# A four-layer graph network on one core: larger first loads on two queues, masks transposed by TensorE, and transfer issues costed anew in the kernel's own schedule

## Chip, cores, metric

One core of one Trainium2 chip. The metric is the device time of one launch in microseconds; lower is better. Each number quoted for a kernel is the median of its runs. The granted TensorE clock is given with each profiled run; all runs of this study were in the fast state (none of them over 1.5% above its kernel's fastest).

## The reference, cut to what matters

32 batches of x (512 nodes, 256 channels, fp32) go through four layers. They share one 512 x 512 adjacency (1 edge in 16, int32). Each layer's result is added to its input and normalised.

```python
def reference(x, adj, ...):
    x = _layernorm(x + _L0_gnn_ref(x, adj, w_qkv, ...))   # 8-head attention, layernorm, FFN, layernorm
    x = _layernorm(x + _L1_gnn_ref(x, W, a, adj))         # 1-head graph attention
    x = _layernorm(x + _L2_gnn_ref(x, adj, W1, W2, W3))   # product attention: (x W1)(x W2)^T
    x = _layernorm(x + _L3_gnn_ref(x, adj, W, a))         # 4-head graph attention, elu
    return x                                              # each attention masked by adj > 0
```

## The kernel before

The kernel does not write its instructions in source order. Every operation is first recorded with a *modelled* cost for each engine that could do it. Then a greedy list scheduler simulates the core and emits the operations in the order in which it placed them. Five batches are open at once. A modelled cost is never executed; it only decides the order of the instructions in each engine's queue, and (where two engines could do an operation) which does it.

```python
AGE = 30.0
LAT = {"PE": 0.3, "DVE": 0.15, "ACT": 0.2, "POOL": 0.25, "SP": 4.0}   # us until a result is usable
# ... (in Plan.run)
            tmin = min(c[0] for c in cands)                  # earliest possible start
            s, o, e = min((c for c in cands if c[0] <= tmin + 0.05),
                          key=lambda c: (not c[1].frees, c[1].graph * AGE - c[1].rank))
            # ...
            if emit:
                o.fn(e)                                      # the instruction is emitted here
            # ...
            for n in o.succ:
                n.ready = max(n.ready, f + LAT[e])
```

The evacuation of a PSUM bank (the copy of PE's result, `ps`, to a tile that other operations read; DVE or ACT may do it) and the layernorm, whose scales come from a chain of four small instructions on POOL (GpSimd):

```python
    def evac(ps, dst, part, out, src=lambda b: b.t, n=512):          # L339 is the copy on ACT
        op({"DVE": cdve(n), "ACT": cact(n)}, lambda e: copy(e, out(dst), src(ps)),
           r=[ps], w=[dst[part]])
    # ... layernorm
            op({"POOL": 1.6}, scales, r=[mv], w=[mv])                # L426 to L429
            # ...
                op({"DVE": 0.325, "ACT": cact(C, 2)}, norm, r=[y[s], mv], w=[dst[s]])   # L438 on ACT
```

Layers 1 and 3 spread their node scores over all partitions by way of DRAM: four stores of rows, then one or two broadcast loads. DVE needs those loads before it can build the matrices that layer 3's products use. Afterwards the products are transposed back:

```python
        def put(e):
            for i in range(4):                               # four DMAs
                nc.sync.dma_start(rd..., rt.t[32 * i:32 * i + n1, :32])
        op({"SP": 0.4}, put, r=[rt], w=[rd])
        for s in range(len(R)):
            op({"SP": 0.2}, lambda e, s=s: nc.sync.dma_start(
                T2(R[s])[:, :hs, :], rd.t[2 * s:2 * s + hs].partition_broadcast(P)), r=[rd], w=[R[s]])
    # ... layer3, after the products (L764 and L770) have been evacuated into sT and oT
        op({"PE": 4 * TR}, back_s, r=[sT], w=[ps_r])         # L785: the sums, transposed back
        # ...
            op({"PE": 4 * TR}, back, r=[oT], w=[ps_t], pre=[t])      # L801: the values
```

The loads at the start, all from SP. The adjacency comes twice: once in 16 block-permuted DMAs for the transposed mask, once in natural rows:

```python
        def block(e, b=b, xZ=xZ):                            # x of one batch, 8 DMAs
            for i in range(4):
                for k in range(KC):
                    nc.sync.dma_start(T2(xZ)[32 * i:32 * i + 32, k, :]..., v[i, :, k])
        op({"SP": 0.8}, block, w=[xZ])
    # ... mask_cols, twice: 8 DMAs of 64 KB, convert on ACT, transpose and compare on DVE
            op({"SP": 0.8}, fn, w=[z])
    # ... mask_rows, per 128 rows
            op({"SP": 0.1}, load(lambda z=z: T2(z)[:, 0, :].bitcast(I32), adj[c * P:(c + 1) * P, :]), w=[z])
            op({"ACT": cact(512) + 0.1}, ... activation(T2(f)[:, 0, :], ..., AF.Copy, accum_out=...), ...)
```

## Time and profile before

| | before |
|---|---|
| median (range), 3 runs | 3114.74 us (3114.32 to 3115.23) |
| profiled span, granted clock | 3116.0 us, 0.983 |
| PE busy | 2967.7 us (95%) |
| start of layer 3's back transposes, first batch | 258.77 us |
| the same, from batch to batch: first six | 97.67, 96.28, 97.28, 97.52, 98.77, 94.8 us |
| the same, settled | 92.4 to 93.0 us; 95.65 and 93.88 once each |

The last rows come from the order of time on PE: I take the start of L785 in each of the 32 batches and subtract. The prediction below shows the page, the table of stretches and the first 60 us.

### The profile page before, as it was taken

To read this page: it belongs to the slowest core of one execution; us is meant where nothing else is said; L and a number is where in the kernel's file an instruction comes from. 1 tells how busy PE (TensorE), PEld (TensorE's weight loads), DVE (VectorE), ACT (ScalarE), POOL (GpSimd) and SP (SyncE) were. 2 spreads that over 40 slices of the span, in tenths; PEclk is the share of its full clock that TensorE was granted. 3 is DMA by queue.
4 is the path that set the end of the run, shared out by engine and by line. 5 is a ranking of instruction groups with operands and counts; after the bars stand their busy time and mean duration, and the time that the engine had idled before them with its cause. 6 is when DMAs were issued, how large, how long until landed. Compare 5 with 4: busy or idle time off the path is not lost. (4 is left out here: it accounts for less than half of the span.)

```text
span 3116.0 us, 49565 instructions
## 1 busy us (share of the span) xinstructions
PE 2967.7 (95%) x17882; PEld 1633.4 (52%) x17882; DVE 2641.2 (85%) x5283; ACT 1693.9 (54%) x3473; POOL 957.2 (31%) x1809
## 2 busy tenths in 40 slices
PE   6899999999999999999999999999999999999885
PEld 2355545555555555455555555555555555555553
DVE  5988888788998888898888998888898888899853
ACT  3555555655555555555555555655555655556342
POOL 0223232232332333333333233333233333233311
PEclk8899999999999999999999999999999999999997
DMA  7001101101011111101101101101101101100000
GB/s 142 12 20 26 38 24 32 38 21 38 25 31 38 29 31 38 31 25 38 38 21 38 38 18 38 38 21 38 38 18 38 38 21 38 38 21 28 31 25 29
DMA packets 205244, 103.76 MB, mean 33 GB/s; under 512 B 154432, under 2 KB 191808, under 8 KB 204992
## 3 DMA queue, kind: packets, MB, share of 16 engines
q1 hardware_dynamic: 204992, 100.52, 12.5%
q8 instruction: 143, 2.34, 0.3%
q14 instruction: 109, 0.89, 0.1%
HBM read 83.36 MB, written 17.12 MB: 32 GB/s over the span
## 5 line engine op out<-in xcount | busy, mean ns | idle before, releaser
L438 ACT ACTIVATE b<-b,t 128x256 f32<-128x256 f32 x768 | 434.2, 600 | 523.4 <-POOL t L429 507.4
L339 ACT ACTIVATE b<-ps 128x512 f32<-128x512 f32 x772 | 430.7, 601 | 361.6 <-PE ps L367 144.1
L485 DVE TENSOR_TENSOR b<-b,maskT 128x1024 f32<-128x1024 f32 x512 | 596.5, 1212 | 16.0 <-ACT b L479 16.0
L479 ACT ACTIVATE b<-ps 128x512 f32<-128x512 f32 x1024 | 527.2, 607 | 128.1 <-PE ps L474 128.1
L426 POOL TENSOR_SCALAR t<-t 128x2 f32<-128x2 f32 x384 | 166.3, 433 | 972.5 <-DVE t L421 873.1
L756 DVE SCALAR_TENSOR_TENSOR b<-b,s,maskT 128x512 f32<-128x512 f32 x512 | 359.1, 741 | 10.7 <-DMA b<-r 10.6
L427 POOL TENSOR_TENSOR t<-t,mhalf 128x2 f32<-128x2 f32 x384 | 339.0, 883 | 32.0
L474 PE MATMUL ps<-b,b 32*128 32x512 f32 x2048 | 301.8, 640 | 21.0 <-ACT b L339 21.0
L497 DVE TENSOR_TENSOR b<-b,b 128x1024 f32<-128x1024 f32 x256 | 297.5, 1210 | 0.0
L419 DVE BATCH_NORM_STATS2 t<-b 128x6 f32<-128x256 f32 x768 | 283.5, 411 | 6.7
L764 PE MATMUL ps<-b,b 128*64 128x512 f32 x1024 | 241.6, 609 | 20.3 <-DVE b L756 20.3
L379 PE MATMUL ps<-b,wqkv_sb 128*128 128x512 f32 x512 | 250.3, 614 | 9.8 <-DMA wqkv_sb<-in_L_gnn_w_qkv_dram 9.8
L407 POOL TENSOR_TENSOR acc<-acc,s 128x32 f32<-128x32 f32 (+2 forms) x96 | 48.2, 502 | 688.2 <-DVE s L524 423.3
L729 PE MATMUL ps<-b,b 128*128 128x257 f32 x1024 | 233.0, 384 | 20.1 <-ACT b L339 20.0
L466 PE MATMUL ps<-b,b 128*32 128x512 f32 x2048 | 247.4, 601 | 0.0
L702 PE MATMUL ps<-b,b 128*128 128x512 f32 x512 | 240.6, 592 | 0.0
L396 PE MATMUL ps<-w_sb,b 128*128 128x256 f32 x1024 | 238.8, 386 | 0.0
L669 PE MATMUL ps<-b,b 128*128 128x257 f32 x1024 | 229.7, 380 | 4.4 <-DVE b L660 4.4
L379 PE MATMUL ps<-b,w_sb 128*128 128x512 f32 x512 | 230.5, 602 | 0.0
L729 PEld LDWEIGHTS ps<-b,b 128*128 128x128 f32 x1024 | 192.3, 190 | 54.4 <-ACT b L339 27.0
L710 DVE CUSTOM_DVE_ANT_0 b<-ps,b 128x512 f32<-128x512 f32 x128 | 87.3, 682 | 149.7 <-ACT b L706 149.7
L669 PEld LDWEIGHTS ps<-b,b 128*128 128x128 f32 x1024 | 193.2, 189 | 38.5 <-issue 5.3
(124 smaller groups left out, 4174.9 us busy)
## 6 DMA issues: line engine op xcount, KB each, us to landing
b<-r SPq DMA_DIRECT2D x64, 512.0 KB
b<-in_x_dram SPq DMA_DIRECT2D x256, 64.0 KB
b<-in_x_dram SPq DMA_DIRECT2D x32, 512.0 KB
out_dram<-b SPq DMA_DIRECT2D x64, 256.0 KB
b<-r SPq DMA_DIRECT2D x32, 256.0 KB
r<-s SPq DMA_DIRECT2D x128, 0.5 KB
r<-s SPq DMA_DIRECT2D x128, 2.0 KB
b<-in_adj_dram SPq DMA_DIRECT2D x16, 64.0 KB
```

What stands on the lines that cost most here:

```text
L339: nc.scalar.activation(dst, src, AF.Copy)
L379: nc.tensor.matmul(ps.t, w.t[:, i, col + k * P:col + (k + 1) * P], T2(xT)[:, i, :], start=(i == 0), stop=(i == KC - 1))
L419: nc.vector.bn_stats(st.t[:, 6 * j:6 * j + 6], T4(y)[:, 2 * s + j, :])
L427: nc.gpsimd.tensor_tensor(mv.t[:, 6:8], mv.t[:, 4:6], mhalf[:, :2], ALU.pow)
L438: nc.scalar.activation(o, i, AF.Identity, bias=b, scale=sc)
L474: nc.tensor.matmul(s[h].t, T2(kT)[r:r + D0, g, c * P:(c + 1) * P], T2(qT)[r:r + D0, g, :], start=True, stop=True)
L479: op({"ACT": cact(512)}, lambda e, c=c, j=j, i=i, s=s, p=p: nc.scalar.activation(T2(p[j][c])[:, i, :], s[2 * j + i].t, AF.Exp, scale=SC0), ...
L485: nc.vector.tensor_tensor(t, t, maskT[c].t.unsqueeze(1).to_broadcast([P, 2, N]), ALU.mult)
L497: op(TT, lambda e, a=p[j][c - 1], b=p[j][c]: nc.vector.tensor_tensor(T2(a), T2(a), T2(b), ALU.add), r=[p[j][c - 1], p[j][c]], w=[p[j][c - 1]])
L669: nc.tensor.matmul(ps.t[:, :C + 1], T2(p[m // 2])[:, m % 2, c * P:(c + 1) * P], hv.t[:, m * (C + 1):(m + 1) * (C + 1)], start=(m == 0), st ...
L729: nc.tensor.matmul(ps_o.t[:, :C + 1], T2(pT)[:, j, m * P:(m + 1) * P], vv()[:, m, :], start=(m == 0), stop=(m == NC - 1))
L756: nc.vector.scalar_tensor_tensor(T2(b)[:, h % 2, :], T2(R[h // 2])[:, h % 2, :], part(1)[:, 0, m, h:h + 1], maskT[m].t, ALU.max, ALU.mult),
```

## The change

Its intent: get the first projection and the masks going sooner with fewer, larger DMAs issued from SP and ACT; load the adjacency once, in natural rows, and have TensorE transpose it; and cost every transfer issue in the schedule at 0.53 us, where the old numbers meant 0.1 (row stores, x) to 0.4. Cut to its core:

```diff
+    DMA = 0.53
 ...
-        op({"SP": 0.4}, put, r=[rt], w=[rd])                  # four row stores, layers 1 and 3
+        op({"SP": 4 * DMA}, put, r=[rt], w=[rd])
 ...
-            op({"SP": 0.2}, lambda e, s=s: nc.sync.dma_start( # row loads
+            op({"SP": DMA}, lambda e, s=s: nc.sync.dma_start(
 ... xs, out, and every constant's load: SP 0.1 / 0.2 / 0.4 -> DMA or n * DMA
-                (nc.sync).dma_start(dst(), src)
+                (nc.scalar if e == "ACT" else nc.sync).dma_start(dst(), src)
 ...
-    def mask_cols(): ...        # 16 block DMAs, 2 DVE transposes, 4 compares
-    def mask_rows(): ...        # 4 row DMAs on SP
+    def masks():
+        for c in range(NC):
+            op({"ACT": DMA}, load(..., adj[c * P:(c + 1) * P, :]), w=[z])
+            op({"ACT": cact(512) + 0.1}, ... parts4(edges(c)), swap(...), AF.Copy, accum_out=...)
+        for m in range(NC):
+            op({"PE": 4 * TR}, tr, r=f, w=[ps])               # 4 transposes of 128x128
+            evac(ps, maskT[m], None, lambda b: b.t)
 ...
-            op({"SP": 0.3}, load(lambda: wqkv_sb.t, rows(w_qkv)), w=[wqkv_sb])
+            op({"ACT": DMA}, load(lambda: wqkv_sb.t, rows(w_qkv)), w=[wqkv_sb])
 ...
             for i in range(4):
-                for k in range(KC):
-                    nc.sync.dma_start(T2(xZ)[32 * i:32 * i + 32, k, :]..., v[i, :, k])
-        op({"SP": 0.8}, block, w=[xZ])
+                nc.sync.dma_start(T2(xZ)[32 * i:32 * i + 32]..., v[i])
+        op({"SP": 4 * DMA}, block, w=[xZ])
```

So the change has two halves: the transfers (what is loaded, by whom, in how many pieces, and the masks) and the model (the numbers in the braces).

More of the change, by code (lines that the diff above doesn't have):

```diff
@@ L505, in layer0 @@
             if g == 0:
-                op({"SP": 0.1}, lambda e: nc.sync.dma_start(
+                op({"SP": DMA}, lambda e: nc.sync.dma_start(
                     T4(xs), x[b].rearrange("(c p) d -> p c d", p=P)), r=[oT[0]], w=[xs])
@@ L823, in fn @@
             with nc.allow_non_contiguous_dma(reason="constants, once"):
-                nc.sync.dma_start(dst(), src)
+                (nc.scalar if e == "ACT" else nc.sync).dma_start(dst(), src)
         return fn
@@ L831, in cols @@
         return a.rearrange("(k p) -> p k", p=P)
-    def mask_cols():
-        for k in range(0, NC, 2):
-            z, f = Buf("B"), Buf("B")
-            def fn(e, k=k, z=z):
-                v = adj.rearrange("(j b) (i k a) -> i b k j a", b=32, k=NC, i=4)
-                for i in range(4):
-                    for q in range(2):
-                        nc.sync.dma_start(
-                            T2(z)[32 * i:32 * i + 32, q, :].bitcast(I32).rearrange(
-                                "p (j a) -> p j a", a=32), v[i, :, k + q])
-            op({"SP": 0.8}, fn, w=[z])
-            op({"ACT": cact(1024)}, lambda e, z=z, f=f: nc.scalar.activation(
-                f.t[:, :2 * N], z.t[:, :2 * N].bitcast(I32), AF.Copy), r=[z], w=[f])
-            z2 = Buf("B")
-            op({"DVE": cdve(1024)}, lambda e, z2=z2, f=f: nc.vector.transpose(
-                z2.t[:, :2 * N], f.t[:, :2 * N]), r=[f], w=[z2])
-            for q in range(2):
-                op({"DVE": 0.35}, lambda e, q=q, k=k, z2=z2: nc.vector.tensor_scalar(
-                    maskT[k + q].t, T2(z2)[:, q, :], 1.0, None, ALU.is_equal), r=[z2], w=[maskT[k + q]])
@@ L855, in mask_rows, with edges, tr @@
-    def mask_rows():
-        cnt = Buf("T")
+    def masks():
+        cnt, f = Buf("T"), [Buf("B"), Buf("B")]
+        def edges(c):
+            return T2(f[c // 2])[:, c % 2, :]
         for c in range(NC):
-            z, f = Buf("B"), Buf("B")
-            op({"SP": 0.1}, load(lambda z=z: T2(z)[:, 0, :].bitcast(I32), adj[c * P:(c + 1) * P, :]),
+            z = Buf("B")
+            op({"ACT": DMA}, load(lambda z=z: T2(z)[:, 0, :].bitcast(I32), adj[c * P:(c + 1) * P, :]),
                w=[z])
-            op({"ACT": cact(512) + 0.1}, lambda e, c=c, z=z, f=f: nc.scalar.activation(
-                T2(f)[:, 0, :], T2(z)[:, 0, :].bitcast(I32), AF.Copy,
-                accum_out=cnt.t[:, c:c + 1]), r=[z], w=[f, cnt])
-            op({"DVE": 0.35}, lambda e, c=c, f=f: nc.vector.tensor_scalar(
-                maskN.t[:, c, :], T2(f)[:, 0, :], 0.0, -BIG, ALU.is_le, ALU.mult),
-                r=[f], w=[maskN])
-            op({"DVE": 0.7}, lambda e, c=c, f=f: nc.vector.tensor_tensor_reduce(
-                T2(f)[:, 1, :], T2(f)[:, 0, :], T2(f)[:, 0, :], 1.0, 0.0, ALU.mult, ALU.add,
-                cnt.t[:, NC + c:NC + c + 1]), r=[f], w=[f, cnt])
+            op({"ACT": cact(512) + 0.1}, lambda e, c=c, z=z: nc.scalar.activation(
+                parts4(edges(c)), swap(T2(z)[:, 0, :].bitcast(I32)), AF.Copy,
+                accum_out=cnt.t[:, c:c + 1]), r=[z], w=[f[c // 2][c % 2], cnt[c]])
+        for m in range(NC):
+            ps = Buf("PS")
+            def tr(e, m=m, ps=ps):
+                for c in range(NC):
+                    nc.tensor.transpose(ps.t[:, c * P:(c + 1) * P],
+                                        edges(c)[:, m * P:(m + 1) * P], ident)
+            op({"PE": 4 * TR}, tr, r=f, w=[ps])
+            evac(ps, maskT[m], None, lambda b: b.t)
+        scr = Buf("B")
+        for c in range(NC):
+            op({"DVE": 0.6}, lambda e, c=c: nc.vector.tensor_scalar(
+                swap(maskN.t[:, c, :]), parts4(edges(c)), 0.0, -BIG, ALU.is_le, ALU.mult),
+                r=[f[c // 2][c % 2]], w=[maskN])
+            op({"DVE": 0.62}, lambda e, c=c: nc.vector.tensor_tensor_reduce(
+                T2(scr)[:, 0, :], edges(c), edges(c), 1.0, 0.0, ALU.mult, ALU.add,
+                cnt.t[:, NC + c:NC + c + 1]), r=[f[c // 2][c % 2]], w=[scr, cnt[NC + c]])
@@ L884, in ffn_weights @@
         for dst, src in ((w1_sb, w1), (w2_sb, w2)):
-            op({"SP": 0.1}, load(lambda d=dst: d.t, rows(src)), w=[dst])
+            op({"SP": DMA}, load(lambda d=dst: d.t, rows(src)), w=[dst])
         for dst, src in ((b1_sb, b1), (g1c, ln1_g), (be1c, ln1_b)):
-            op({"SP": 0.1}, load(lambda d=dst: d.t, cols(src)), w=[dst])
+            op({"SP": DMA}, load(lambda d=dst: d.t, cols(src)), w=[dst])
         for dst, src in ((g1_sb, ln1_g), (g2_sb, ln2_g), (be2_sb, ln2_b)):
-            op({"SP": 0.1}, load(lambda d=dst: d.t, src.partition_broadcast(P)), w=[dst])
+            op({"SP": DMA}, load(lambda d=dst: d.t, src.partition_broadcast(P)), w=[dst])
         for dst, src in ((be1r, ln1_b), (b2r, b2)):
-            op({"SP": 0.1}, load(lambda d=dst: d.t[:, :C], src.partition_broadcast(P)), w=[dst])
+            op({"SP": DMA}, load(lambda d=dst: d.t[:, :C], src.partition_broadcast(P)), w=[dst])
         ps = Buf("PS")
@@ L922, in put @@
                     nc.sync.dma_start(c1p.t[i:i + 1, k, :], bf(i)[0:1, :])
-            op({"SP": 0.2}, put, r=[parts[i]], w=[c1p])
+            op({"SP": 2 * DMA}, put, r=[parts[i]], w=[c1p])
     def score_weights(w, src, a, heads):
@@ L931, in score_weights @@
         for j in range(4):
-            op({"SP": 0.4}, load(lambda j=j: w.t[32 * j:32 * j + 32, :, :C],
+            op({"SP": DMA}, load(lambda j=j: w.t[32 * j:32 * j + 32, :, :C],
                                  src.rearrange("(q a) d -> a q d", a=32)), w=[w])
-        op({"SP": 0.4}, load(lambda: wr.t[:, :KC * C].rearrange("p (k d) -> p k d", k=KC), rows(src)),
+        op({"SP": DMA}, load(lambda: wr.t[:, :KC * C].rearrange("p (k d) -> p k d", k=KC), rows(src)),
            w=[wr])
-        op({"SP": 0.4}, load(lambda: a_sb.t[:, :n], a.partition_broadcast(P)), w=[a_sb])
+        op({"SP": DMA}, load(lambda: a_sb.t[:, :n], a.partition_broadcast(P)), w=[a_sb])
         def fn(e):
@@ L951, in put @@
                                   sc.t[:, :KC * e3].rearrange("p (k e) -> p k e", k=KC))
-        op({"SP": 0.4}, put, r=[sc], w=[dr])
+        op({"SP": DMA}, put, r=[sc], w=[dr])
         def get(e):
@@ L958, in get @@
                                       dr.t.rearrange("(q a) e -> a q e", a=32))
-        op({"SP": 1.6}, get, r=[dr], w=[w])
+        op({"SP": 4 * DMA}, get, r=[dr], w=[w])
     def product_weights():
-        op({"SP": 0.1}, load(lambda: w3_sb.t, rows(l2_w3)), w=[w3_sb])
+        op({"SP": DMA}, load(lambda: w3_sb.t, rows(l2_w3)), w=[w3_sb])
         wt = []
@@ L966, in product_weights @@
             w, t = Buf("B"), Buf("B")
-            op({"SP": 0.1}, load(lambda w=w: w.t[:, :KC * C].rearrange(
+            op({"SP": DMA}, load(lambda w=w: w.t[:, :KC * C].rearrange(
                 "p (k d) -> p k d", k=KC), rows(src)), w=[w])
@@ L999, in block @@
             for i in range(4):
-                for k in range(KC):
-                    nc.sync.dma_start(
-                        T2(xZ)[32 * i:32 * i + 32, k, :].rearrange("p (j a) -> p j a", a=32),
-                        v[i, :, k])
-        op({"SP": 0.8}, block, w=[xZ])
+                nc.sync.dma_start(
+                    T2(xZ)[32 * i:32 * i + 32].rearrange("p k (j a) -> p k j a", a=32), v[i])
+        op({"SP": 4 * DMA}, block, w=[xZ])
         xs = Buf("B")
         if b == 0:
-            mask_cols()
+            masks()
             ffn_weights()
@@ L1012 @@
             product_weights()
-            mask_rows()
             plan.stage = 3
@@ L1021 @@
         for s in range(2):
-            op({"SP": 0.1}, lambda e, b=b, s=s, xs=xs: nc.sync.dma_start(
+            op({"SP": DMA}, lambda e, b=b, s=s, xs=xs: nc.sync.dma_start(
                 out[b].rearrange("(c p) d -> p c d", p=P)[:, 2 * s:2 * s + 2, :],
```

## The prediction

> **What bounds the kernel now.** I read the page first: the busy shares, then the 40 slices.
>
> ```profile
> span 3116.0 us, 49565 instructions
> PE 2967.7 (95%) x17882; PEld 1633.4 (52%) x17882; DVE 2641.2 (85%) x5283; ACT 1693.9 (54%) x3473; POOL 957.2 (31%) x1809
> PE   6899999999999999999999999999999999999885
> DVE  5988888788998888898888998888898888899853
> DMA  7001101101011111101101101101101101100000
> ```
>
> TensorE is the bound from the third slice to the last but two; transfers matter in the first slice alone (share 7 tenths, then 0 or 1). So almost everything this change could win lies in PE's idle time: 3116.0 - 2967.7 = 148 us. The table of stretches says where those sit.
>
> ```profile
> core 0: us, PE busy (x) PEld busy (x) DVE busy (x) ACT busy (x) POOL busy (x), PEclk, DMA share, GB/s
> 0.00:100.00 100.00, 68.79 (x341) 30.17 (x341) 64.23 (x90) 48.76 (x98) 10.22 (x58) 0.86 0.59 116
> 100.00:200.00 100.00, 85.05 (x407) 49.01 (x411) 84.44 (x212) 48.82 (x98) 26.02 (x55) 0.91 0.04 9
> ...
> 700.00:800.00 100.00, 95.56 (x601) 55.06 (x594) 84.72 (x169) 52.69 (x111) 32.12 (x56) 0.97 0.11 30
> 800.00:900.00 100.00, 98.67 (x598) 52.12 (x597) 88.98 (x172) 57.82 (x118) 30.65 (x55) 1.00 0.11 30
> ...
> 3000.00:3100.00 100.00, 72.50 (x385) 40.13 (x378) 45.72 (x109) 23.43 (x51) 9.25 (x31) 0.86 0.09 30
> ```
>
> PE idles 31 us in the first 100, 15 in the second, 18 from 300 to 800, about 1.3 per 100 from 800 to 2800, and some 53 in the last 216 (the drain of the last batches). Then the order of time in the first 60 us:
>
> ```profile
> 4.89 0.49 SPq L824 DMA_DIRECT2D wqkv_sb<-in_L_gnn_w_qkv_dram  x1
> 5.42 9.80 SPq L842 DMA_DIRECT2D b<-in_adj_dram  x16
> 9.82 9.07 PE L379 MATMUL ps<-b,wqkv_sb 128*128 128x512 f32 x16 [9.82 <-DMA wqkv_sb<-in_L_gnn_w_qkv_dram]
> 32.14 4.09 SPq L824 DMA_DIRECT2D b<-in_adj_dram  x4
> 40.58 0.63 ACT L863 ACTIVATE b<-b 128x512 f32<-128x512 int32 x1 [20.73 <-DMA b<-in_adj_dram]
> 41.83 0.50 PEld L474 LDWEIGHTS ps<-b,b 32*128 32x128 f32 x2 [20.78 <-ACT b L339]
> 45.54 6.57 PE L396 MATMUL ps<-wqkv_sb,b 128*128 128x256 f32 x16
> ```
>
> The story is in the ACT line. ACT's queue is in order; the conversion of the natural adjacency rows stands in it ahead of two evacuations of the first q and k. Those rows are queued on SP behind 51 other issues and are sent only at 32 to 36 us, so ACT sits 20.7 us, and PE with it from 21.8 to 41.8. The schedule put it there because it counted 0.1 us for an issue; the trace shows 0.31 to 0.51 us each.
>
> **What the Trainium skill says.** "DMA: Bandwidth & Descriptors", section "Issuing engines are not separate DMA queues": transfers from different issuing engines interleave on the same 16 engines; a second issuer saves only issue time. No run here shows two issuers yet. It fits that what can be won is the 0.5 us per issue, which this trace has. Same page, Specifications: 512 B or more per descriptor for line rate. The trace agrees: in the one-microsecond windows, the 128-byte packets of x and adjacency move at 106 to 141 GB/s, the 3072-byte rows of w_qkv at 353 (7 to 9 us). "TensorE: Matmul & The Clock Gate", section "What's actually happening": an idle PE is throttled to half clock and needs about 3.4 us of activity to be released. The trace agrees: the first fp32 matmuls take up to 1190 ns against 592 later, and the granted clock stands at 0.5 from 25 to 50 us.
>
> **The change part by part.**
>
> *The start.* From the changed instruction order, ACT's queue opens with w_qkv and four 256 KB row loads of the adjacency, without waits: about 0.7 to 3.3 us. SP sends x in four issues, the fourth waiting for w_qkv's landing (they share a semaphore lane). Bytes: x 0.52 MB at about 0.16 MB/us (122 GB/s at a DMA share of 0.77) = 3.3 us; w_qkv 0.79 MB and adjacency 1.05 MB at 0.353 MB/us = 5.2 us; w1 and two bias rows compete, some 1 us. From 1.7 us, with landing latency about 1 us, the last adjacency chunk is there near 11 us. ACT converts it (0.62 + 0.19) by 11.8; the four earlier table load and conversions are hidden. PE: 16 transposes, 1.04 us per eight warm (L801), twice that cold: about 3.5 us, to 15.3. The b1 product, 1.05, to 16.4. DVE meanwhile: four maskN of about 0.45, one reduction of 0.7, two x transposes of 0.65: done near 14.5, no wait. Four projections at 1.78 us each (7.1 us for four, from L379 later) to 23.5, two scores operations 2.2, then the v projection from about 26.5 to 30.5, now at the full clock. Before, that same v projection (L396) ran from 45.54 to 52.11. So the path is about 20 us earlier. PE begins later (11.8 against 9.8) and still gains, since the 20 us wait is gone. DVE can keep up: its first mask multiply needs only the l1 score weights done, whose vector lands near 21 us (its issue waits for the DVE casts near 17), and six reductions of 0.47: near 24 us, against 45.1 before. **-20 us.**
>
> *DVE and PE work.* DVE loses two 1.25 us transposes and four compares (1.39 in all), and its maskN takes a permuted view: within 1 us of neutral. PE gains 16 transposes, counted above.
>
> *100 to 200 us.* One wait of 10.2 us there is PE for DVE's add (L501) in a phase with DVE at 8 to 10 tenths. The new order starts the third batch's layer 0 ahead of the first batch's layer 1, which gives PE something to do, but DVE has only some 4 us idle between 110 and 150. **-4 us.**
>
> *200 to 800 us.* The old order becomes periodic (316 matmuls per batch) at matmul 2265 of 10134, the new one at 1313 of 10150. In the old transient PE waits at L785, the back-transposes of the sums, on ACT's evacuation: 16.3 us in five batches. I count half of that as won: **-8 us.**
>
> *The period.* Before, the period is 92.6 us with two small waits, L729 0.7 us and L785 0.57. In the new period three further operations (a q/k projection and two others) stand between the sums' last product and L785, which covers the second: 0.57 x 22 = 13 us at most; the chain score to exponential to transposes has two fewer projections behind it (3.9 us instead of 7.7), which the trace's 2.4 us of slack with the x-transpose in DVE's way makes just enough. **-6 us**, and **+8 us** as a reserve for waits in a new order that I do not see.
>
> *x loads later on.* 128 issues fewer, 0.5 us each, and SP is idle most of a period; its waits never reach PE (L448's 1.7 us wait delays nothing PE needs at once). **0.** *The drain*: the same chain (four row stores, r loads of 3 to 4 us, masks, products); 19 instead of 22 PE operations follow the last but one batch. **0.**
>
> Sum: -20 - 4 - 8 - 6 + 8 = -30: 3114.7 - 30 = **3085 us**.
>
> **The rivals.** *(a) The start shifts but DVE takes it back.* DVE is at 10.0 of 10 from 60 to 110 us; if it is the bound there for other reasons than its late start, the 20 us shrink. For: the saturation. Against: between 0 and 57 us DVE was idle for over 30 us, waiting on PE and ACT. It would leave 3100 us. *(b) A new wait per batch in the changed order.* One wait of 1 us per period costs 28 us and eats all else: 3110 us; 2 us: 3140. For: the order is wholly different and the schedule is greedy. Against: its model is truer than before, DVE has 11% slack and ACT 43%. *(c) The order removes most of the transient and both small waits*: -20 - 10 - 16 - 16 = 3053 us. For: periodic 950 matmuls sooner. Against: the wait at L729 has the same neighbours as before. *(d) The shared queues make the start slower*: small packets of x delay the adjacency, and PE waits for all four chunks before anything: each microsecond costs one; 5 us late gives 3090.
>
> **Range and chances.** The start is the surest term, -15 to -24; transient and period together could be anything from -30 to +20. **Predicted 3085 us, 8 in 10 between 3063 and 3106.** Faster by over 2% needs under 3052: rival (c) in full, 0.04. Slower by over 2% needs a wait of 3 us in each batch: 0.02. Within 2%: 0.94.
>
> **What would show it.** Right: first PE matmul (transposes) at 11 to 13 us, v projection of the first batch near 26 to 31 us, no PE wait over 5 us between; PE idle in the first 100 us near 15 instead of 31; 300 to 800 us at 97% or better; L785 absent from PE's waits, L729 still there near 0.7 us a batch; PE busy total up by 2 us. Wrong: a row of PE waits once per 92 us at one line; DVE full and PE waiting on it from 40 to 100 us; or adjacency landing after 15 us.

## The result, and the profile after

Changed kernel 3018.69 us (3016.89 to 3022.36, 4 runs), before 3114.53 us (3112.89 to 3115.23, 4 runs) beside it. Ratio 0.9695, 95% interval 0.9678 to 0.9711. A ratio here is the mean time of one kernel's runs over that of the other's of the same rounds, so it is not quite the ratio of the medians quoted. The gain is 96 us where 30 were predicted, outside the range.

The page of the changed kernel (span, busy time, PE's row in 40 slices):

```profile
span 3020.5 us, 49063 instructions
...
PE 2947.4 (98%) x17898; PEld 1633.3 (54%) x17898; DVE 2635.2 (87%) x5277; ACT 1688.5 (56%) x3475; POOL 866.8 (29%) x1809
...
PE   8999999999999999999999999999999999999885
```

and its table of stretches, columns as in the prediction:

```profile
0.00:100.00 100.00, 87.93 (x430) 39.30 (x434) 79.12 (x116) 56.17 (x111) 10.16 (x58) 1.00 0.54 105
100.00:200.00 100.00, 92.39 (x518) 53.85 (x513) 87.54 (x210) 53.37 (x110) 30.72 (x60) 0.95 0.04 12
700.00:800.00 100.00, 100.00 (x599) 55.69 (x596) 88.60 (x176) 57.81 (x118) 27.53 (x56) 1.00 0.12 30
800.00:900.00 100.00, 100.00 (x588) 55.19 (x588) 89.53 (x188) 58.00 (x119) 32.60 (x73) 1.00 0.14 35
```

The first line answers to 68.79, the second to 85.05. The last two are the news: PE has no idle time left there, where 1.3 to 4.4 us in 100 were idle. The line numbers of the changed kernel are one higher than before's in the part that matters (L785 is L786, L339 is L340, L438 is L439, L429 is L430, L379 is L380, L396 is L397).

The start, in order of time, went nearly as predicted: adjacency rows issued from ACT, PE's first transposes at 9.13 us (earlier than the predicted 11 to 13), the v projection at 26.11 us (26.5) where before had it at 45.54.

```profile
1.20 2.61 ACTq L825 DMA_DIRECT2D b<-in_adj_dram  x4
...
9.13 1.70 PE L853 MATMUL ps<-ident,b 128*128 128x128 f32 x3 [9.13 <-ACT b L845]
...
15.41 8.85 PE L380 MATMUL ps<-b,wqkv_sb 128*128 128x512 f32 x16
...
26.11 3.72 PE L397 MATMUL ps<-wqkv_sb,b 128*128 128x256 f32 x16
```

Where the 95.5 us between the two profiled spans came from, by the start of layer 3's back transposes in each batch (L785 or L786):

| part of the run | before | after | gain |
|---|---|---|---|
| to the first batch's | 258.77 | 243.03 | 15.7 |
| the next 6 batches | 582.32 | 552.96 | 29.4 |
| the next 21 batches | 1949.54 (92.84 each) | 1899.20 (90.44 each) | 50.3 |
| the last 4 batches | 307.93 | 308.23 | -0.3 |
| from there to the end | 17.44 | 17.08 | 0.4 |

So by this marker four fifths of the gain lie after the start, where the change alters no transfer but x in four DMAs instead of eight. The marker belongs to one batch, and the new order may do more or less work of other batches ahead of it, so the parts are rough. PE's idle time, cut at the same places, falls from 46.2 to 19.7 us in the first part, from 18.7 to 0 in the second, from 30.6 to 0 in the third, and rises from 52.8 to 53.4 in the last two: 75.2 of the 95.5 us, two thirds of them after the start. The waits of PE tell whom it waited for. Before, from 300 to 800 us (columns: line waiting, what for, us in total, times, longest):

```profile
PE ps L785 <- ACT b L339: 16.3, 5, 4.0
PE ps L729 <- ACT b L339: 1.9, 4, 0.6
```

and before, from 1000 to 2500 us:

```profile
PE ps L729 <- ACT b L339: 13.4, 16, 2.1
PE ps L785 <- ACT b L339: 9.1, 16, 0.6
```

The same view of the changed kernel from 500 to 2500 us lists no wait of PE at all.

**What holds ACT's evacuation.** Here is one settled batch of before (start, duration, engine, line, and in brackets the idle time and its releaser):

```profile
1513.66 0.60 ACT L438 ACTIVATE b<-b,t 128x256 f32<-128x256 f32 x1 [2.38 <-POOL t L429]
...
1514.17 0.58 ACT L339 ACTIVATE b<-ps 128x512 f32<-128x512 f32 x1
1514.65 0.59 ACT L438 ACTIVATE b<-b,t 128x256 f32<-128x256 f32 x1
...
1515.14 2.52 ACT L339 ACTIVATE b<-ps 128x512 f32<-128x512 f32 x5
1516.26 7.23 PE L729 MATMUL ps<-b,b 128*128 128x257 f32 x32 [0.69 <-ACT b L339]
...
1580.01 1.09 ACT L438 ACTIVATE b<-b,t 128x256 f32<-128x256 f32 x2 [3.45 <-POOL t L429]
1581.01 3.01 ACT L339 ACTIVATE b<-ps 128x512 f32<-128x512 f32 x6
1581.64 0.66 PE L785 MATMUL ps<-ident,b 128*128 128x128 f32 x4 [0.57 <-ACT b L339]
```

The page calls the culprit "ACT L339", but ACT is not slow, it is *held*: in front of the evacuations its queue has a normalisation that waits 2.4 or 3.5 us for POOL's scales. Because POOL is late, the normalisations run just when the evacuations are due: at 1514 us one stands between the first evacuation and the rest, at 1580 us two run first (1.09 us), then six evacuations in a bunch, and PE goes on when the first of these is done. The Trainium skill ("Perfetto Trace Analysis", section "Tensor Engine Instruction (MATMUL, LD_WEIGHTS)") says that the execution queues of ACT, DVE and GpSimd are strictly first in, first out. The trace agrees: at 1581 us the evacuations start one after another only after the held L438. Why POOL is late shows in the same trace. Its four instructions take 1.4 us before 1513.66 (1512.23 to 1513.63), but 4.5 us before 1580.01 (1575.52 to 1579.98), while DVE multiplies by the mask (L485, from 1574.17 to 1582.19). Over the whole run one L426 takes 0.19 us beside DVE's L419 and 1.05 us beside its L485 (medians of those that overlap one of them for over 80% of their time). 113 of before's 384 chains take over 3 us, and 62 of the changed kernel's: the order also decides beside which DVE work POOL's chain falls. No run isolates what that is worth.

The corresponding place in the changed kernel:

```profile
1505.85 1.09 ACT L439 ACTIVATE b<-b,t 128x256 f32<-128x256 f32 x2 [2.46 <-POOL t L430]
1509.85 1.09 ACT L439 ACTIVATE b<-b,t 128x256 f32<-128x256 f32 x2 [2.92 <-POOL t L430]
...
1513.54 2.62 ACT L340 ACTIVATE b<-ps 128x512 f32<-128x512 f32 x5 [2.59 <-PE ps L771]
1514.33 5.32 PE L380 MATMUL ps<-b,w_sb 128*128 128x512 f32 x12
...
1519.48 0.60 PE L786 MATMUL ps<-ident,b 128*128 128x128 f32 x4
```

ACT still waits for POOL, but four microseconds earlier, when PE needs nothing from it. When the products end it is waiting for PE, as it should. And 5.3 us of projections of another batch (L380) stand between the products and the back transposes, so even a late evacuation would not stop PE. Over the whole run ACT's wait for POOL fell from this (before)

```profile
ACT b L438 <- POOL t L429: 507.4, 265, 23.4
```

to this (after):

```profile
ACT b L439 <- POOL t L430: 244.3, 132, 10.4
```

**Why five waits cost more than their length.** In the first six periods a wait of 3 to 4 us at L785 also cost clock. Before, around 550 us:

```profile
550.00 1.11 PE L785 MATMUL ps<-ident,b 128*128 128x128 f32 x4 [3.07 <-ACT b L339]
551.76 1.70 PE L801 MATMUL ps<-ident,b 128*128 128x128 f32 x8
```

and one microsecond of the table of stretches there, 0.50 being the granted clock:

```profile
550.00:551.00 1.00, 1.00 (x5) 1.00 (x6) 0.00 (x0) 1.00 (x3) 0.00 (x0) 0.50 0.00 0
```

The granted clock is 1.00 up to 549 us, 0.84 in the next microsecond, 0.50 from 550 to 553 and 1.00 again from 554. L785 takes 1.11 us instead of 0.66 and L801 1.70 instead of 1.04. In the six periods together PE is idle 18.7 us and works 14.7 us at half clock, which costs at most half of that, 7.4 us. Both are gone in the changed kernel: 26.1 of the 29.4 us gained there. The other 3.3 us were not split further.

### The profile page after: what moved, and what is told of

Its sections match the earlier page's. It is cut to its first block, busy times and chain, and to the rows that moved or that the text cites.

```text
span 3020.5 us, 49063 instructions
## 1 busy us (share of the span) xinstructions
PE 2947.4 (98%) x17898; PEld 1633.3 (54%) x17898; DVE 2635.2 (87%) x5277; ACT 1688.5 (56%) x3475; POOL 866.8 (29%) x1809
## 4 chain that ended last, share of the span: by engine, by line
PE 92%; DVE 4%; issue 1%; DMA 1%; ACT 1%; POOL 1%; SPq 1%; DVEq 0%; ACTq 0%; POOLq 0%
PE ps L380 15%; PE ps L397 11%; PE ps L467 9%; PE ps L475 8%; PE ps L611 8%; PE ps L765 7%; PE ps L730 7%; PE ps L703 7%; PE ps L670 7%; PE ps L771 4%; PE ps L368 2%; PE ps L722 2%; PE ps L536 1%; PE ps L701 1%; PE ps L802 1%
## 5 line engine op out<-in xcount | busy, mean ns | idle before, releaser
L340 ACT ACTIVATE b<-ps 128x512 f32<-128x512 f32 x772 | 434.9, 602 | 497.2 <-PE ps L380 186.9
L439 ACT ACTIVATE b<-b,t 128x256 f32<-128x256 f32 x768 | 425.6, 597 | 255.9 <-POOL t L430 244.3
L427 POOL TENSOR_SCALAR t<-t 128x2 f32<-128x2 f32 x384 | 135.2, 352 | 845.0 <-DVE t L422 777.8
L475 PE MATMUL ps<-b,b 32*128 32x512 f32 x2048 | 300.4, 640 | 0.0
L408 POOL TENSOR_TENSOR acc<-acc,s 128x32 f32<-128x32 f32 (+2 forms) x96 | 77.3, 806 | 637.8 <-DVE s L525 378.1
L380 PE MATMUL ps<-b,wqkv_sb 128*128 128x512 f32 x512 | 248.1, 609 | 0.0
L397 PE MATMUL ps<-w_sb,b 128*128 128x256 f32 x1024 | 245.6, 388 | 1.4 <-ACT b L340 1.4
L380 PE MATMUL ps<-b,w_sb 128*128 128x512 f32 x512 | 235.5, 603 | 2.5 <-ACT b L340 2.5
L730 PE MATMUL ps<-b,b 128*128 128x257 f32 x1024 | 228.5, 380 | 0.4 <-ACT b L340 0.4
L670 PEld LDWEIGHTS ps<-b,b 128*128 128x128 f32 x1024 | 195.8, 192 | 45.4 <-issue 10.6
L397 PEld LDWEIGHTS ps<-w_sb,b 128*128 128x128 f32 x1024 | 190.0, 191 | 53.8 <-issue 30.0
L408 POOL TENSOR_TENSOR acc<-acc,t 128x2 f32<-128x2 f32 (+2 forms) x128 | 37.9, 308 | 598.7 <-DVE t L789 325.7
```

Source lines behind the costliest of these rows:

```text
L340: nc.scalar.activation(dst, src, AF.Copy)
L380: nc.tensor.matmul(ps.t, w.t[:, i, col + k * P:col + (k + 1) * P], T2(xT)[:, i, :], start=(i == 0), stop=(i == KC - 1))
L397: nc.tensor.matmul(two(ps)[:, j, :], T2(xT)[:, i, c * P:(c + 1) * P], w.t[:, i, col:col + C], start=(i == 0 and row is None), stop=(i == K ...
L439: nc.scalar.activation(o, i, AF.Identity, bias=b, scale=sc)
L475: nc.tensor.matmul(s[h].t, T2(kT)[r:r + D0, g, c * P:(c + 1) * P], T2(qT)[r:r + D0, g, :], start=True, stop=True)
L670: nc.tensor.matmul(ps.t[:, :C + 1], T2(p[m // 2])[:, m % 2, c * P:(c + 1) * P], hv.t[:, m * (C + 1):(m + 1) * (C + 1)], start=(m == 0), st ...
```

## The experiments

Each was run for three rounds beside before (e3 has 12 times and e6 19, the others 4); all outputs were correct. The table gives the result of each with the parts of the run (columns as rows above: to the first batch's back transposes, next 6, mean of the next 21, last 4).

| kernel | median us | ratio to before (95%) | first | next 6 | each of 21 | last 4 |
|---|---|---|---|---|---|---|
| before | 3114.53 | 1 | 258.8 | 582.3 | 92.84 | 307.9 |
| changed | 3018.69 | 0.9695 (0.9678 to 0.9711) | 243.0 | 553.0 | 90.44 | 308.2 |
| e1 put cost only | 3040.85 | 0.9744 (0.9727 to 0.9760) | 265.1 | 553.7 | 90.44 | 306.0 |
| e2 changed, old row costs | 3063.21 | 0.9814 (0.9797 to 0.9830) | 246.8 | 562.2 | 91.63 | 309.8 |
| e3 before, x in four | 3125.95 | 1.0014 (1.0005 to 1.0023) | 256.4 | 586.5 | 93.15 | 309.8 |
| e4 changed, x in eight | 3027.71 | 0.9701 (0.9685 to 0.9717) | 247.9 | 553.0 | 90.44 | 307.9 |
| e5 model only | 3030.15 | 0.9719 (0.9702 to 0.9735) | 263.9 | 542.6 | 90.44 | 305.3 |
| e6 transfers only | 3124.55 | 1.0023 (1.0016 to 1.0030) | 255.9 | 578.8 | 93.27 | 307.7 |
| e7 hold back transposes | 3334.19 | 1.0693 (1.0675 to 1.0711) | 262.7 | 617.6 | 100.64 | 320.8 |
| e8 hold norms | 3142.62 | 1.0081 (1.0064 to 1.0098) | 260.0 | 592.3 | 93.15 | 313.8 |
| e9 issue 0.30 | 3074.86 | 0.9852 (0.9836 to 0.9869) | 257.5 | 555.7 | 92.25 | 309.0 |
| e10 issue 0.60 | 3014.14 | 0.9658 (0.9642 to 0.9674) | 241.4 | 545.2 | 90.52 | 310.4 |
| e11 issue 0.80 | 3026.04 | 0.9697 (0.9681 to 0.9713) | 241.7 | 560.4 | 90.65 | 300.7 |
| e12 POOL 2.3 | 3036.46 | 0.9730 (0.9714 to 0.9746) | 243.2 | 555.8 | 91.02 | 306.9 |

The medians come from several calls, in which before itself stood at 3114.5 to 3121.5 us; only ratios compare across calls. The expectations in us were written for a call in which before takes about 3114.

**My theory** after reading the traces: nearly all of the gain is the model's, not the transfers'. The cost of the row stores places what hangs on them later, so other batches' PE work goes ahead of layer 3's back transposes, and the evacuations come in time. **The rival**: fewer, larger transfers (x in four instead of eight, one adjacency load) relieve SP or the DMA engines and thereby the waits.

### e1: the row stores' cost alone, in the kernel before

```diff
+    DMA = 0.53
-        op({"SP": 0.4}, put, r=[rt], w=[rd])
+        op({"SP": 4 * DMA}, put, r=[rt], w=[rd])
```

> The kernel before with one number changed: the modelled SP cost of the four row stores ahead of the r loads, 0.4 to 2.12 us. No transfer changes. Theory S (the schedule's picture of this one wait decides the order of a batch, and the order decides the time): the instruction order becomes the changed kernel's period, so a batch takes 90.4 us instead of 92.6 once settled, the first 60 us keep their 20 us PE wait; about 3114 - 2.15 x 22 - 20 for a shorter transient = 3043 us, between 3030 and 3060. Theory T (the gain comes from fewer and larger transfers on two queues): 3114 us, within 5.

One number that no engine ever executes takes 2.6% off the kernel, within theory S's interval. Every engine runs as many instructions as in before (17882 matmuls, 3473 on ACT, 5283 on DVE); only their order differs. The settled period is 90.44 us, that of the changed kernel. Its start is before's: the wait of PE for the first evacuations is still there, at the same place.

```profile
45.87 3.77 PE L475 MATMUL ps<-b,b 32*128 32x512 f32 x4 [24.07 <-ACT b L340]
```

### e2: the changed kernel with the old row costs

```diff
-        op({"SP": 4 * DMA}, put, r=[rt], w=[rd])
+        op({"SP": 0.4}, put, r=[rt], w=[rd])
-            op({"SP": DMA}, lambda e, s=s: nc.sync.dma_start(   # row loads
+            op({"SP": 0.2}, lambda e, s=s: nc.sync.dma_start(
```

> The changed kernel with the old modelled costs of the row stores (0.4) and r loads (0.2) alone; every transfer is as in the changed kernel. Theory S: the batch has the old order again, 92.6 us per batch, PE waits at the L786 and L730 lines are back; what stays is the earlier start, 16 us, and some 5 us of a transient that ends earlier: 3090 us, between 3080 and 3100. Theory T: about 3019 us.

Taking just the row costs back gives up 1.2 of the 3.05%: 91.63 us a batch, with 9.7 us of waits at the back transposes in 1000 to 2500 us (16 times, one each batch), and a longer second phase. It does not return to before's 92.84, and with 3063.21 us theory S's 3080 to 3100 was missed; the wait at the layer 2 products stays away. So the row stores' cost is enough (e1), but other issue costs also steer away from the old order.

### e3 and e4: x in four or eight DMAs, order unchanged

```diff
 # e3, in before (cost 0.8 kept)          # e4, in the changed kernel (cost 4 * DMA kept): the reverse
-                for k in range(KC):
-                    nc.sync.dma_start(T2(xZ)[32 * i:32 * i + 32, k, :]..., v[i, :, k])
+                nc.sync.dma_start(T2(xZ)[32 * i:32 * i + 32]..., v[i])
```

> The kernel before with x loaded in four transfers instead of eight, the modelled cost kept, so the order on every engine is the same. Theory S: 3114 us, within 4. Theory T (128 fewer issues on SP let the stores and r loads go earlier): 20 us or more faster.

> The changed kernel with x loaded in eight transfers again, the modelled cost kept, so the order is the same. Theory S: 3019 us plus at most 5 at the start (x lands later by the issue of four more transfers). Theory T: 20 us or more slower than the changed kernel.

Both kernels keep their order, so these isolate the 128 saved issues. Before with x in four is 0.14% slower (4.5 us, just outside theory S's 4), the changed kernel with x in eight stands at 0.9701 against 0.9695, and its profiled start is 4.8 us later (247.86 against 243.03), as expected. So either way the effect is within 0.15%, and the rival's 20 us are not there; the prediction's "x loads later on: 0" holds.

### e5 and e6: the model alone, the transfers alone

```diff
 # e5: before, only the numbers
-        op({"SP": 0.8}, block, w=[xZ])           # and mask_cols' 8 DMAs
+        op({"SP": 8 * DMA}, block, w=[xZ])
-        op({"SP": 0.4}, put, ...)   -  {"SP": 0.2} / 0.1 / 0.3 / 0.4 / 1.6 elsewhere
+        op({"SP": 4 * DMA}, put, ...)   +  DMA per issue elsewhere
 # e6: the changed kernel, every issue cost back at the old number
-            op({"ACT": DMA}, load(..., adj rows))
+            op({"ACT": 0.1}, load(..., adj rows))
-        op({"SP": 4 * DMA}, put, ...)            # and so on
+        op({"SP": 0.4}, put, ...)
```

> The kernel before with every issue on SP counted as 0.53 us in the schedule's model, and no transfer, queue or mask changed. Theory S says the model alone does nearly all: a settled batch of 90.44 us, no wait of 20 us near 22 us because the first q and k evacuations now stand ahead of the adjacency rows in ACT's queue. w_qkv goes out behind 24 other issues, so the first projection starts near 16 us instead of 9.8 (before) and the v projection near 28 us (26.1 in the changed kernel, 45.5 before). In ratio to the kernel before: 0.971 to 0.975 (3025 to 3035 us on a chip where before takes 3114 to 3121). Theory T (the loads and the transposed masks make the start): the start gives at most half of its 16 us, ratio 0.977 or more.

> The changed loads, queues and masks with all the old modelled costs. Theory S: the start of the changed kernel (v projection of the first batch near 26 us), but the old order of a batch: PE waits at L785 in every batch, 91.6 to 92.6 us per batch, and a transient of some batches at 96 to 98. Ratio to before 0.983 to 0.995. Theory T: ratio 0.970.

With e5 and e6 the two halves stand in a square: neither 1, model alone 0.9719, transfers alone 1.0023, both 0.9695. **The model makes 2.8% of the 3.05%, and the transfers alone make nothing.** The rival has fallen. But e6 also missed its theory S (0.983 to 0.995): the early start was expected to last. And what the transfers add to the model is hardly clear of noise, as the intervals of e5 and of the changed kernel overlap.

The square also shows what the transfers are worth under the new costs: at the first batch's marker 243.0 (changed) against 263.9 (e5), 20.9 us. That this is near the predicted 20 is chance: in e5 the v projection starts at 29.62 us (expected near 28), so of the 19.4 us by which it came earlier the model alone makes 15.9. And e5 reaches its period at once and the changed kernel only after two batches (553.0 against 542.6 for the next six), and its drain is 2.9 us longer, so 7.4 us remain (the spans of 3027.9 and 3020.5 us).

Why e6 fails to keep its early start is again a held queue. Its v projection is early (26.61 us), but then, in order of time:

```profile
40.03 1.30 DVE L448 STREAM_TRANSPOSE b<-b 128x512 f32<-128x512 f32 x2 [8.37 <-DMA b<-in_x_dram]
...
51.21 5.24 PE L466 MATMUL ps<-b,b 128*32 128x512 f32 x16 [17.04 <-DVE b L485]
```

DVE's queue has x's transposes of a later batch (waiting for a transfer that the old model thinks cheap), then layer 3's score weights up to 50 us, ahead of the mask multiplies (L485) that PE needs. So PE waits 17 us there, instead of 20 us for ACT. This is read from the trace and was not tested by a run.

### e7 and e8: curing the waits one at a time

If single waits are the cost, moving a few instructions in before's order should win what they cost. In both, the emission holds some operations (and any that share a buffer with them) back; the plan itself is before's.

```diff
-                o.fn(e)
+                self.emit(o, e)
 # e7: layer 3's back_s and back on PE are held until three other PE operations have been emitted
 # e8: layer 0's ACT norms are held while layer 2's scores and transposes are emitted
```

> The kernel before, its schedule unchanged, except that in emission the sum and output transposes of layer 3 (L785, L801) are put behind the three PE operations that follow them (one transpose group, two projections). Nothing else moves but what depends on them. If PE's waits at L785 are the cost: a settled batch goes from 92.57 to about 91.4 us (0.57 of wait and as much again of split groups and switches, as e2 with this wait alone has 91.61 against 90.44), the transient batches from 97.5 to about 93: some 1.15 x 21 + 4 x 6 = 48 us less, ratio 0.984. If the waits are only where a deficit of another kind shows, PE waits elsewhere by the same amount and the ratio is 0.997 or more.

> The kernel before, except that ACT's normalisations of layer 0's last layernorm (L438), where they stand between the scores and the transposed probabilities of another batch, are put behind the evacuations that follow. If ACT's queue, held by a normalisation that waits for POOL, is what makes PE wait at L729: that wait is gone, a settled batch takes about 91.6 us instead of 92.57, ratio 0.992, and the batch of 95.65 us is gone too. If the evacuations are late for another reason: ratio 0.998 or more, L729 still waits 0.7 us.

e7 is 6.9% **slower**; neither of its theories allowed for that. The wait at the back transposes is gone, and PE waits elsewhere for ACT's evacuations (L371 is the evacuation, L761 the layer 2 products, L411 the projections), from 1000 to 2500 us:

```profile
PE ps L761 <- ACT b L371: 63.3, 15, 4.3
PE ps L411 <- ACT b L371: 28.2, 15, 1.9
```

I read it so, without a run that tests it: delayed back transposes delay everything after them in the other queues, which stand in an order made for the earlier time. The granted clock of the run fell to 0.959 as well. So e7 does not show that the wait at L785 was worth nothing, only that this way of removing it costs more.

e8 did remove the wait at the layer 2 products as expected, and yet is 0.8% slower: the wait at the back transposes grew to 0.8 us a batch, as the same view shows,

```profile
PE ps L817 <- ACT b L371: 13.0, 16, 0.8
```

and one group of layer 0 scores became about 1 us longer (eight matmuls take 2.09 us instead of 1.07), its exponentials on ACT now standing behind the delayed norms. A wait removed by hand in one queue came back in another. So two repairs by hand failed, and the order as a whole succeeded; which of its differences is needed, no run takes apart.

### e9 to e12: is 0.53 good because it is true?

In the first 60 us of before most issues take 0.31 to 0.51 us (median 0.49, a few held for up to 2.5), and in a row of them on SP one starts every 0.53 us. The four row stores that before counted at 0.4 us together take 1.9 us (each 0.26 to 0.71). Is a true model the cause, or did the scheduler, being greedy, happen upon a good order? Only the constant was changed in the changed kernel.

```diff
-    DMA = 0.53
+    DMA = 0.3        # e9;  0.6 in e10;  0.8 in e11
```

> The changed kernel with the modelled cost of one transfer issue 0.3 us instead of 0.53 (transfers, queues and masks as changed). Only the order of the instructions differs. Theory A (the order is better because the modelled issue cost is near the true one, 0.31 to 0.51 us, median 0.49, so the time worsens smoothly with the distance from it): 0.3 is 60% of the true cost, half way from 0.53 to the old numbers of the row stores (0.1 each): 3040 to 3070 us. Theory B (a greedy scheduler falls into one of a few orders; which one is luck, and a nearby number can give a bad or a better order): I see before the run that this order settles late, and in a pattern like that of the kernel before: period about 92 to 93 us, 3080 to 3120 us.

> As the last, with 0.6 us. Theory A: 13% above 0.53, still as near to the truth with the landing of the store's data counted: 3010 to 3030 us, within 0.5% of the changed kernel. Theory B: the order has a different period from that at 0.53 (seen in the instruction order), so the time may move by more than 0.5% either way: below 3005 or above 3035.

> As the last, with 0.8 us; the order does not become periodic at all. Theory A: 60% too high, so worse by about as much as 0.3 is: 3040 to 3070 us. Theory B: anything; if it is as fast as the changed kernel or faster (under 3025), a true cost is not what the gain needs, only a late enough placing of the row loads' consumers. A third theory (a): more modelled wait on the row loads is always better, since it puts more PE work between the layer 3 products and their back transposes: 2990 to 3018.

0.3 gives 0.9852: neither theory's interval (3040 to 3070 and 3080 to 3120) quite holds 3074.86; by its ratio to a before of 3114.5 it would be 3068 us, just in theory A's. Half of the gain is lost, at the start (a wait like e6's 17.0 us is back: 19.7 us at the same products) and in the settled batches (92.25 us on average). 0.6 gives 0.9658, the fastest of all and inside theory A's interval, with a period of 90.52 us; 0.8 gives 0.9697, the changed kernel's ratio and outside theory A's interval, with periods that alternate between 86.1 and 95.7 us. So **at the three values from 0.53 to 0.8 nothing is lost, and at 0.3 half is**: three unlike orders end within 0.2 us a batch of each other, and in all three PE is busy 500.00 of 500 us from 1500 to 2000. That may be the floor that PE's own work sets; e12 below shows that a busy PE alone does not prove it. The accuracy theory holds from below only; that 0.8, 60% too high, costs nothing speaks against accuracy as such, and for "late enough". So does the kernel's own `LAT`, which adds 4.0 us to every SP operation: the stores' data counted as usable 4.4 us after the first issue began with the old number and 6.1 us with the new one, while in before's trace the issues take 1.9 us and SP waits at most 1.1 us more for the stores before it issues a row load. The new number is truer for SP's time and less true for that wait. The third theory (more is always better) fails as well, at 3026.04.

```diff
-            op({"POOL": 1.6}, scales, r=[mv], w=[mv])
+            op({"POOL": 2.3}, scales, r=[mv], w=[mv])        # e12
```

> The changed kernel with the modelled cost of the layernorm's scale chain on POOL 2.3 us instead of 1.6 (by the trace its four instructions take 1.98 us busy, and 2.2 to 2.4 us from the first's start to the last's end). ACT still waits for POOL 244 us in the changed kernel. Theory A (truer costs give better orders): fewer ACT waits for POOL (under 150 us), PE idle in the first 200 us less; PE is already at 100 of 100 from 200 to 2800 us, so the gain can only be in the group splits and the ends: 2995 to 3018 us. Theory B (greedy luck): anywhere within 1.5% of the changed kernel, as likely above as below.

The four POOL instructions are 1.98 us busy by the groups (0.352 + 0.885 + 0.313 + 0.430), so 2.3 with the hand-overs was meant to be truer than 1.6. In fact no single number is true: from the first's start to the last's end the chain takes 1.4 to 4.5 us in the changed kernel (median 1.74, mean 2.12). The kernel became 0.36% **slower** than the changed one by the two ratios, and ACT's wait for POOL rose, from 244.3 us, as 134 chains instead of 62 took over 3 us:

```profile
ACT b L439 <- POOL t L430: 529.0, 171, 9.2
```

Theory A's expectation (fewer such waits, 2995 to 3018 us) failed in both parts. So a number nearer the mean is no gain in itself. The other 285 us of ACT waiting hardly touch PE, whose only waits from 1000 to 2500 us are four of 0.4 us: what counts is not how long ACT waits, but whether somebody needs it then. The remaining 0.6 us a batch over the changed kernel is not idle time of PE. With the groups on PE laid side by side over four settled batches (from the start of one to the start of the next), layer 0's scores (L475) take 36.2 us instead of 34.3 and the layer 2 products (L730, in nine groups instead of four) 29.6 instead of 28.2; all together it is 2.6 us. At 1631 us sixteen score matmuls take 3.9 us, at 1664 us 1.93. In the short group four of them start within 0.02 us of each other; in the long one they come, after the first few, one or two at a time. PE counts as busy throughout, so such a wait hides in "busy".

The fastest kernel is e10. It beats before by 3.4%, and the changed kernel's ratio by 0.4%. The two were not run in one call, though their intervals do not overlap.

## Why the prediction was wrong

The step that failed is the settled order: the prediction had it at -6 and +8 us, as if the new order were worth no more than the old. It won 50.3 us in 21 batches, because both of PE's small waits went (30.6 us of idle time, now 0) and PE's groups became shorter (some 18 us). The transient, at -8 for 29.4, failed in size. By its own sum (-20 start, -4 from 100 to 200 us, -8 from 200 to 800 us, -6 period, +8 reserve, 0 x loads, 0 drain):

- **The start, -20, and -4 for 100 to 200 us: right.** The v projection came 19.4 us earlier (26.11 against 45.54), with no PE wait over 0.2 us between the first transposes and it; PE idle in the first 100 us fell by 19.1 to 12 (predicted 15), in the second 100 by 7.4 to 7.6. By the first batch's back transposes only 15.7 us show. What the prediction did not see is how little of it the transfers make: under the new costs without them (e5) the v projection starts at 29.62 us, and with them under the old costs (e6) only 2.9 us are left at the first batch's marker.
- **"I count half of that as won: -8 us": failed in size, at 29.4.** Two faults. I took 16.3 us of waits as all there was, while in the six periods PE was idle 18.7 us and also worked 14.7 us at half clock after the waits of 3 to 4 us. My own prediction had quoted the Trainium skill on this ("TensorE: Matmul & The Clock Gate") for the start and not applied it here. And halving it was a hedge with no view behind it: the waits went altogether.
- **"The period ... -6 us", and "+8 us as a reserve": failed, at -50.3 for 21 batches.** This is the largest miss. I had the two waits right (0.57 and 0.7 us a batch, 13.4 + 9.1 us in 1000 to 2500), had seen that three operations now cover L785, and gave L729 up because "the wait at L729 has the same neighbours as before". Its neighbours on PE were the wrong ones to look at: what held it was the norm ahead of it *in ACT's queue*. Comparing the order on ACT would have shown that. I had also read PE's idle time from 800 to 2800 us as 1.3 in 100; it is 31.1 in 2000, or 1.6. With both waits gone, 22.5 us in 1500, or 1.4 us a batch, are explained. Of the remaining 1.0 of the 2.4 us a batch, some 0.1 is one spell of half clock (3.4 us), and the larger part is about 0.9 us of PE operations that run slightly longer in before where the order splits a group in two or three (L367 in three groups instead of two) or changes from one kind to another. That is read from operations laid side by side; no run took it apart.
- **The reserve itself** assumed that an unseen new order is as likely to bring waits as to lose them. The changed order brought none in the settled batches. e7 shows that such waits do come, so the doubt was not foolish; but the evidence in hand (a modelled 0.4 us for what the trace shows as 1.9) pointed one way, and I used it for the start alone.
- **x loads and drain, 0 and 0: right** (e3, e4: 0.14% and 0.06%; drain -0.3 and +0.4 us of gain).
- **"PE busy total up by 2 us": wrong, it fell by 20.3**, though 16 matmuls were added; in e1, with before's instructions on before's engines, it fell by 31.1. A matmul's recorded end is modelled, as the same section of "Perfetto Trace Analysis" says, and durations stretch at a lower clock and in split groups. So "busy" was not a floor: the prediction's 148 us of idle time was not all that could be won. Of the 95.5 us, 75.2 are idle time and 20.3 are busy time.
- **Rivals.** Rival (c), "the order removes most of the transient and both small waits", named the right step; it was put at 3053 us and 0.04. Its terms (-20, -10, -16, -16) are each in the right direction, and still short, since both the clock and the shorter groups were left out. (a), (b) and (d) did not happen.

What stays open: what the 0.9 us of slightly longer operations per batch consists of, how much POOL's slower chains are worth, and which of the differences between the two orders are needed.

## What to carry to other kernels

In a kernel whose order comes from a cost model, ask first what a changed number does to the order, and price that in the steady state; the visible rewrite may be the smaller half, and one experiment that changes the numbers alone separates the two. When PE waits for an engine that is half idle, read that engine's own queue for the instruction that held it, and do not mend single waits by hand in a dense order. After such a change try neighbouring values too: the best constant need not be the true one, but here a cost well below the measured duration was the expensive side. And compare the length of like groups on PE as well as its idle time: a PE counted as busy can still be waiting.

## What the Trainium skill lacked or had wrong

- "DMA: Bandwidth & Descriptors", section "Issuing engines are not separate DMA queues", says that the time to initiate a DMA is "usually small relative to the DMA itself". For the row stores of 0.5 KB or 2 KB it is not small: issuing four takes 1.9 us, and SP waits at most 1.1 us more for the stores before it issues a row load. The section gives no figure for the issue on this chip and does not name this case.
- "Perfetto Trace Analysis", section "Tensor Engine Instruction (MATMUL, LD_WEIGHTS)", has the strict order of ACT's queue, but not how it shows: the wait is charged to the evacuation that came late (L339), while the bracket on the instruction before it in ACT's queue names POOL (2.38 and 3.45 us). Following one step back along the queue is what finds it.
- No page says by how much PE's busy time can move when only the order of the operations changes: in e1, with the same 17882 matmuls, it is 2936.6 us instead of 2967.7.
